# Attention on one Trainium2 core: the inverse deviation of the next image on GpSimd in pieces, half of one value product a round earlier, two norms moved towards each other

## The chip, the cores and the metric

The program runs on one core of a Trainium2 chip. The metric is the device time of one execution in microseconds, taken as the median of several runs. All data are float32.

## What is computed

The input is 8 images of 128 channels by 32 x 32 places. Two layers follow each other; the change lies in the attention of the first.

```python
# x: (8, 128, 32, 32); 8 heads of 16 channels
h = ln_c(x)                                  # over channels: (x - mean) / sqrt(var + 1e-6)
q, k, v = h @ wq.T, h @ wk.T, h @ wv.T
weights = softmax(einsum('bhwnd,bxynd->bnhwxy', q, k) * scale, axis=-1)   # over y only
x = x + einsum('bnhwxy,bxynd->bhwnd', weights, v)
t = x as 1024 tokens of 128
t = t + spectral(ln_t(t))                    # 16 causal filters, ln_t over channels, eps 1e-5
x = x + deformable_conv(ln_c(x))
t = t + experts(ln_t(t))                     # 8 experts, 2 per token
```

The softmax runs over rows of 32 keys, so each query has 32 sums per head.

## The kernel before

**Order.** `metaformer_kernel` first bounds the scores; with the given weights it takes `attention_bounded`, which works with no maximum in the softmax. It writes x1 to DRAM (`x1d`). Then `spectral_and_second_layer` does the spectral filters of image pairs on TensorE and runs the second layer of finished images behind them. Inside the attention the order on every engine is written by hand: `at(round_no, order, ...)` collects pieces, which are issued sorted by round, then by order, then as they were listed. An engine executes its own pieces strictly in that order, and waits at the head of its queue.

**Rounds and units.** An image has 8 units: 4 quarters of 256 queries (`qc`) by 2 groups of 4 heads (`hg`). A unit takes four rounds, so image b begins in round `first` = 32 b and there are 256 rounds. I number them 0 to 255, and call a round's place in its unit its place 0, 1, 2 or 3 (the round number modulo 4). For the unit that starts in round t0:

- Rounds t0 to t0+3, order 0: `scores`, 8 matmuls into the one PSUM tile `s` (L601; the pool has one buffer, 4 banks) and the exponential on ScalarE into `e` (L606). Order 1: `add_tiles` on GpSimd adds the two key tiles to `t` (L615).
- Round t0+5, order 4: `sums`, 16 matmuls into `z` (L622), and on VectorE `reciprocals` (L629).
- Round t0+6, order 2.5: `spread_out`, 4 matmuls into `rb` (L636).
- Rounds t0+6 to t0+9, order 3: `divide` on VectorE, `e` times `rb` (L643).
- Rounds t0+8 to t0+11, order 2: `values`, 8 matmuls into `av` (L653).
- After every second unit `take` copies `av` to `o` (L663, round t0+11), and `results` (L670, round t0+12) transposes it back, so `po` falls in place 0.

As the unit of t0+8 comes two units later, one round of the steady state holds on TensorE: scores, values and one more thing: `po` or a projection of the next image in place 0 (four units of eight each), `z` in place 1, `rb` in place 2, a projection in place 3.

**The next image.** Its rows are loaded and transposed (`tokens`, ScalarE copies to `xt`), normalised, transposed again (`channels`) and projected (`keys`, `queries`, `key_values`), in rounds of the image before, at order 5.5 and 6. `layer_norm_pieces` makes the 21 pieces of the norm: `stats` 0 to 7 on VectorE (L79, L80), `guess` (L84 to L89) and three `newton` (L93 to L96) for the inverse deviation by integer guess and Newton steps, `offset` (L99, tile `lp_nm`), all on VectorE and 128 x 8 numbers each, then `norm` 0 to 7 on ScalarE (L104), which need `lp_nm` and `lp_y`. The list `norm_at` gives their rounds: for images 2 to 7 the stats in 29 to 22 rounds ahead of `first`, `guess` in -22, `newton` in -21, -21, -20, `offset` in -20, four `norm` in -19 and four in -18. Image 1 has a list of its own.

**The first group.** `FirstGroup.pieces` uses the same pieces at order 7 to normalise x1 of images 0 and 1 for the spectral stage (tiles `xc` and `ht`), in rounds 224 + 8 and on for image 0 (`guess` 16, `offset` 20, `norm` 20 to 23) and ten rounds later for image 1, so that its last `norm` come after the last scores.

**Elsewhere.** `inverse_std` does the same computation for later groups of the spectral stage, there with the Newton steps on GpSimd (L757 to L762).

Of the kernel before, what the change touches and what calls it, by code (L numbers as in the profile page):

```python
# [12 lines left out]
I32 = mybir.dt.int32  # L13
AF = mybir.ActivationFunctionType
ALU = mybir.AluOpType
# [3 lines left out]
P = 128  # L19
# [3 lines left out]
NT = T // P  # L23
# [41 lines left out]
def layer_norm_pieces(nc, pool, src, dst, eps):  # L65

    t = {}

    def stats(i):
        if i == 0:
            for name, shape in (
                ("st", [P, NT, 6]), ("mv", [P, NT, 2]), ("v", [P, NT]), ("y", [P, NT]),
                ("w", [P, NT]), ("nm", [P, NT]),
            ):
                t[name] = pool.tile(shape, F32, tag=f"lp_{name}", name=f"lp_{name}")
            t["b"] = pool.tile([P, NT], I32, tag="lp_b", name="lp_b")
        nc.vector.bn_stats(t["st"][:, i, :], src()[:, i, :])  # L79
        nc.vector.bn_aggr(t["mv"][:, i, :], t["st"][:, i, :])  # L80

    def guess():
        v, y = t["v"], t["y"]
        nc.vector.tensor_scalar(v, t["mv"][:, :, 1], eps, None, ALU.add)  # L84
        nc.vector.tensor_scalar(t["b"], v.bitcast(I32), 1, None, ALU.logical_shift_right)
        nc.vector.tensor_scalar(
            y.bitcast(I32), t["b"], -1, 0x5F3759DF, ALU.mult, ALU.add
        )
        nc.vector.tensor_scalar(v, v, -0.5, None, ALU.mult)  # L89

    def newton():
        v, y, w = t["v"], t["y"], t["w"]
        nc.vector.tensor_mul(w, y, y)  # L93
        nc.vector.tensor_mul(w, w, v)
        nc.vector.tensor_scalar(w, w, 1.5, None, ALU.add)
        nc.vector.tensor_mul(y, y, w)  # L96

    def offset():
        nc.vector.scalar_tensor_tensor(  # L99
            t["nm"], t["mv"][:, :, 0], -1.0, t["y"], ALU.mult, ALU.mult  # L100
        )

    def norm(i):
        nc.scalar.activation(  # L104
            dst()[:, i, :], src()[:, i, :], AF.Identity, bias=t["nm"][:, i : i + 1],
            scale=t["y"][:, i : i + 1],
        )

    return (
        [partial(stats, i) for i in range(NT)] + [guess, newton, newton, newton, offset]  # L110
        + [partial(norm, i) for i in range(NT)]
    )
# [379 lines left out]
def attention_bounded(ctx, tc, ident, x, x1d, given, begin_group):  # L492
# [8 lines left out]
    nc = tc.nc  # L501
# [17 lines left out]
    for i in range(2):  # L519
        v = cp.tile([P, NT, VB], F32, name=f"vt{i}")  # L520
# [123 lines left out]
            e, e, un["rb"].unsqueeze(2).to_broadcast([P, NH, 2, QU]), ALU.mult  # L644
        )

    def values(img, un, r, qrt):
        hg = un["at"][1]
        if hg == 0 and r == 0:
            qrt["av"] = rp.tile([P, 512], F32, tag="av", name="av")  # L650
        for c in range(2):
            for j in range(NH):
                nc.tensor.matmul(  # L653
                    qrt["av"][32 * j : 32 * j + 32, 0:QU],
                    img["v"][:, 2 * r + c, P * hg + 32 * j : P * hg + 32 * j + 32],
                    un["e", r][:, j, c, :],
                    start=(hg == 0 and r == 0 and c == 0),
                    stop=(hg == HG - 1 and r == 3 and c == 1), skip_group_check=True,
                )
# [24 lines left out]
    def at(round_no, order, do, *args):  # L684
        work.append((round_no, order, len(work), do, args))

    def spread_rounds(pieces, rounds):
        for piece, round_no in zip(pieces, rounds):
            at(round_no, 6, piece)

    for b in range(B):
        img = {}
        first = 4 * UNITS * b
        project = [
            (keys, img, 0, 0), (keys, img, 0, 1), (queries, img, 0, 0),
            (keys, img, 1, 0), (keys, img, 1, 1), (queries, img, 1, 0),
            (key_values, b, img, 0), (key_values, b, img, 1),
            (queries, img, 0, 1), (queries, img, 1, 1),
        ]
        if b == 0:  # L700
            turn = {"tokens": (0, 0)}
            project_at = (-1, -1, -1, 1, 2, 3, 7, 8, 11, 12)
        else:
            project_at = [first + n for n in (-12, -9, -5, -4, -1, 3, 4, 7, 11, 12)]
            if b == 1:
                turn = {"load": 0, "tokens": (4, 6)}
                norm_at = (5,) * 4 + (7,) * 4 + (8, 8, 9, 9, 9) + (10,) * 4 + (11,) * 4
            else:
                turn = {"load": first - 36, "tokens": (first - 30, first - 26)}
                norm_at = [first - n for n in (  # L710
                    29, 28, 27, 26, 25, 24, 23, 22, 22, 21, 21, 20, 20, 19, 19, 19, 19, 18, 18, 18, 18
                )]
            turn["channels"] = (first - 17, first - 13)
        if b:
            at(turn["load"], 6, load, b)
            spread_rounds(
                layer_norm_pieces(nc, sb, lambda i=img: i["xt"], lambda: given.ht, 1e-6), norm_at
            )
            for par in range(2):
                at(turn["channels"][par], 5.5, channels, par)  # L720
        for par in range(2):
            at(turn["tokens"][par], 5.5, tokens, img, par)
        for step, when in zip(project, project_at):
            at(when, 6, *step)
        for qc in range(QC):
            qrt = {}
            for hg in range(HG):
                un = {"at": (qc, hg)}
                t0 = first + 4 * (HG * qc + hg)
                for r in range(4):  # L730
                    at(t0 + r, 0, scores, img, un, r)
                    at(t0 + r, 1, add_tiles, un, r)
                    at(t0 + 5, 4, sums, un, r)
                    at(t0 + 6 + r, 3, divide, un, r)
                    at(t0 + 8 + r, 2, values, img, un, r, qrt)
                at(t0 + 5, 5, reciprocals, un)
                at(t0 + 6, 2.5, spread_out, un)
            at(t0 + 11, 5, take, qrt)
            at(t0 + 12, 6, results, b, img, qc, qrt)
# [427 lines left out]
class FirstGroup:  # L1167
# [19 lines left out]
    def pieces(self, pool):  # L1187

        got = [(14, self.read), (3, partial(self.load, 0)), (4, partial(self.load, 1))]
        for n in range(2):  # L1190
            pieces = layer_norm_pieces(
                self.nc, pool, lambda n=n: self.ur[n], lambda n=n: self.ur[n], 1e-5
            )
            rounds = [*range(8, 21), *(20 + i // 2 for i in range(8))]
            got += [(r + 10 * n, piece) for r, piece in zip(rounds, pieces)]
        return got


# [258 lines left out]
def metaformer_kernel(  # L1457
# [25 lines left out]
    with tc.If(bounded > P - 1) as branch:  # L1483
        with ExitStack() as part:
            attention_bounded(part, tc, ident, x, x1d, given, begin.pieces)
# [66 lines left out]
```

## Time and profile before

| | |
|---|---|
| median of 3 runs | 3130.27 us (3128.75 to 3132.58) |
| the profiled execution | 3137.39 us, span 3135.6 us |
| attention: first scores to first filter matmul (`pu`) | 27.9 to 996.6 us |
| granted TensorE clock, mean | 0.947 |

The span is what the profile sees of its one execution, 1.8 us less than that execution's time; this execution lies 7.1 us above the median. A timeline line reads: start, duration, engine, line, operation, out<-in, size, count, and in brackets how long the engine was idle before and what released it. A float32 matmul appears as two records, so the 8 matmuls of `scores` are x16. PEld is TensorE's weight load.

### The profile page before, as it was taken

How to read it: one execution, taken by the hardware profiler on the slowest of the kernel's cores; microseconds unless marked ns; L12 is line 12 of the kernel's file. 1: busy time of each engine (PE TensorE's matmuls, PEld its weight loads, DVE VectorE, ACT ScalarE, POOL GpSimd, SP SyncE). 2: the span in 40 equal slices, each digit the busy share in tenths (PEclk: the TensorE clock that was granted, in tenths of full speed). 3: DMA queues.
4: the chain of work that ended last, by engine and by line, in shares of the span. 5: the costliest groups of instructions: out<-in, count | busy, mean ns of one | idle time of the engine just before them, and what ended most of it. 6: DMA issues, size and time to landing. Idle time of an engine off the chain costs nothing.

```text
span 3135.6 us, 45294 instructions
## 1 busy us (share of the span) xinstructions
PE 2793.4 (89%) x18896; PEld 1713.5 (55%) x18896; DVE 1464.0 (47%) x3035; ACT 978.7 (31%) x1198; POOL 957.2 (31%) x800
## 2 busy tenths in 40 slices
PE   7989889989986999999899899899899989899506
PEld 3545445545443666666566566566566656566202
DVE  4788788788786200000522440333522143332487
ACT  4666666666653111112112112212112211111100
POOL 4767667667663200000301300300300030300230
PEclk9999999999998999999999999999899999999758
DMA  0000000000001422210614411511611341610540
GB/s 25 2 15 15 1 15 15 2 15 9 2 28 40 115 61 65 76 48 27 201 41 124 124 34 41 171 58 58 184 34 48 107 121 34 191 51 14 175 146 14
DMA packets 177011, 199.80 MB, mean 64 GB/s; under 512 B 17236, under 2 KB 135188, under 8 KB 176800
## 3 DMA queue, kind: packets, MB, share of 16 engines
q1 hardware_dynamic: 147328, 134.97, 14.4%
q0 software_dynamic: 16800, 55.59, 5.8%
q10 hardware_dynamic: 12672, 6.29, 0.7%
q8 instruction: 150, 2.46, 0.3%
q14 instruction: 61, 0.50, 0.1%
HBM read 128.88 MB, written 67.92 MB: 63 GB/s over the span
## 4 chain that ended last, share of the span: by engine, by line
PE 54%; DVE 4%; another core or an unknown queue 3%; issue 1%; DMA 1%; ACT 1%; POOL 0%; ACTq 0%; POOLq 0%; DVEq 0%
PE pu L1355 33%; PE po L1343 15%; PE p_e L1076 3%; DVE x L1058 2%; PE p_g L1002 1%; DVE x L1082 1%; DMA tab<-gs 1%; PE p_out L1093 0%; PE p_out L1096 0%; PE p_turn L905 0%; PE p_l L1120 0%; DMA g<-tab,cn_idx 0%; ACT us L1359 0%; PE p_ut L1299 0%
## 5 line engine op out<-in xcount | busy, mean ns | idle before, releaser
L1359 ACT COPY us<-pu 128x512 f32<-128x512 f32 x512 | 300.1, 586 | 1382.0 <-PE pu L1355 1228.9
L615 POOL TENSOR_TENSOR t<-e 128x1024 f32<-128x1024 f32 x256 | 620.1, 2424 | 312.2 <-ACT e L606 312.2
L1355 PE MATMUL pu<-teto,ur 128*128 128x512 f32 (+3 forms) x2048 | 603.1, 438 | 51.3 <-ACT us L1359 40.1
L643 DVE TENSOR_TENSOR e<-e,rb 128x2048 f32<-128x2048 f32 x256 | 572.7, 2277 | 87.9 <-PE rb L636 85.6
L606 ACT ACTIVATE e<-s 128x2048 f32<-128x2048 f32 x256 | 480.9, 1878 | 293.2 <-PE s L601 291.6
L1355 PEld LDWEIGHTS pu<-teto,ur 128*128 128x128 f32 x2048 | 390.2, 192 | 330.7 <-issue 201.5
L1343 PE MATMUL po<-us,mf 128*128 128x128 f32 (+2 forms) x2048 | 530.8, 383 | 0.0
L601 PE MATMUL s<-q,k 32*128 32x256 f32 x4096 | 303.0, 411 | 37.0 <-ACT e L606 30.1
L1355 PE MATMUL pu<-teto,ht 128*128 128x512 f32 x992 | 292.2, 438 | 23.0 <-ACT us L1359 23.0
L653 PE MATMUL av<-e,vt 128*32 128x256 f32 x4096 | 283.2, 395 | 28.7 <-DVE e L643 23.8
L1043 POOL DMA_INDIRECT g<-tab,cn_idx x192 | 185.0, 964 | 377.2 <-DMA tab<-gs 194.3
L1355 PE MATMUL pu<-teto,xc 128*128 128x512 f32 x992 | 290.1, 435 | 2.9 <-issue 2.9
L1058 DVE SCALAR_TENSOR_TENSOR x<-g,w,x 128x128 f32<-128x128 f32 x704 | 250.3, 357 | 60.0 <-DVE x L1058 24.1
L601 PEld LDWEIGHTS s<-q,k 32*128 32x128 f32 x4096 | 190.2, 189 | 157.8 <-ACT e L606 101.2
L1355 PEld LDWEIGHTS pu<-teto,xc 128*128 128x128 f32 x992 | 188.7, 191 | 157.0 <-issue 116.9
L1343 PEld LDWEIGHTS po<-us,mf 128*128 128x128 f32 x2048 | 272.1, 193 | 4.1 <-issue 3.9
L757 POOL TENSOR_SCALAR rs_v<-rs_v 128x8 f32<-128x8 f32 x18 | 4.4, 246 | 875.2 <-DVE rs_b L755 875.2
L1082 DVE SCALAR_TENSOR_TENSOR x<-p_e,gates,x 128x128 f32<-128x128 f32 x512 | 177.6, 350 | 187.0 <-PE p_e L1076 170.8
L1355 PEld LDWEIGHTS pu<-teto,ht 128*128 128x128 f32 x992 | 189.6, 192 | 135.7 <-issue 67.0
L653 PEld LDWEIGHTS av<-e,vt 128*32 128x32 f32 x4096 | 108.9, 111 | 164.3 <-issue 72.7
L629 DVE RECIPROCAL r<-z 128x256 f32<-128x256 f32 x64 | 112.4, 1757 | 110.8 <-PE z L622 77.4
L1076 PE MATMUL p_e<-ew,tc 128*128 128x512 f32 x256 | 134.8, 633 | 14.0 <-DVE x L1082 8.9
(235 smaller groups left out, 1809.6 us busy)
## 6 DMA issues: line engine op xcount, KB each, us to landing
tab<-gs SPq DMA_DIRECT2D x168, 256.0 KB
mf<-mfd SPq DMA_DIRECT2D x48, 512.0 KB
teto<-in_phi_o SPq DMA_DIRECT2D x63, 256.5 KB
teto<-in_phi_e SPq DMA_DIRECT2D x63, 256.0 KB
mfd<-mf SPq DMA_DIRECT2D x16, 512.0 KB
tab<-gs ACTq DMA_DIRECT2D x24, 256.0 KB
xc<-in_x SPq DMA_DIRECT2D x8, 512.0 KB
x1d<-xt SPq DMA_DIRECT2D x8, 512.0 KB
```

What stands on the lines that cost most here:

```text
L601: nc.tensor.matmul(s[:, j, c, :], img["k"][rows, hg, 2 * r + c, :], q[rows, qc * QU : (qc + 1) * QU], start=True, stop=True,)
L606: nc.scalar.activation(e.rearrange("p j c q -> p (j c q)"), s.rearrange("p j c q -> p (j c q)"), AF.Exp, scale=float(HD) ** -0.5,)
L615: nc.gpsimd.tensor_add(t, e[:, :, 0, :], e[:, :, 1, :])
L643: nc.vector.tensor_tensor(e, e, un["rb"].unsqueeze(2).to_broadcast([P, NH, 2, QU]), ALU.mult)
L653: nc.tensor.matmul(qrt["av"][32 * j : 32 * j + 32, 0:QU], img["v"][:, 2 * r + c, P * hg + 32 * j : P * hg + 32 * j + 32], un["e", r][:, j, ...
L1043: nc.gpsimd.indirect_dma_start(out=g, out_offset=None, in_=rows, in_offset=bass.IndirectOffsetOnAxis(ap=idx[:, i, tap : tap + 1], axis=0),)
L1058: nc.vector.scalar_tensor_tensor(x3[:, i, :], fetched[n][:, k * C : (k + 1) * C], w[:, i, tap, k : k + 1], (tok if tap + k == 0 else x3)[: ...
L1076: nc.tensor.matmul(pe, tc[:, i * P : (i + 1) * P], self.ew[:, grp * 4 : grp * 4 + 4, :].rearrange("d e c -> d (e c)"), start=True, stop=True,)
L1082: nc.vector.scalar_tensor_tensor(x3[:, i, :], pe[:, k * C : (k + 1) * C], gate[:, i, grp * 4 + k : grp * 4 + k + 1], x3[:, i, :], ALU.mult ...
L1343: self.nc.tensor.matmul(out, lhsT, rhs, start=bank not in group["opened"], stop=last, skip_group_check=True)
L1355: nc.tensor.matmul(pu[:, i * P : HT], group["ur"][n][:, src * 4 + i, :], flt[:, 0 : HT - i * P], start=(i == 0), stop=(i == 3),)
L1359: nc.scalar.copy(us[:, n, :], pu)
```

## The change

Three edits.

1. `guess`, `newton` and `offset` are issued on GpSimd. The guess no longer shifts the bits: it multiplies the integer by -0.5 and adds the constant in one operation, so the tile `lp_b` goes; `offset` becomes two operations. On VectorE these were 17 operations (4 + 12 + 1), on GpSimd they are 17 (3 + 12 + 2). The rounds for images 2 to 7 change: stats in pairs in -29, -28, -25, -24, `guess` in -24, `newton` in -23, -22, -22, `offset` in -22, `norm` in pairs in -21 to -18. Image 1 keeps its rounds.
2. `values` takes the key tiles it is to do. For r = 1 the first half (4 matmuls) moves from round t0+9 to the end of round t0+8 (order 6.5, behind projections and `po`).
3. In the first group, image 1's norm follows image 0's by 4 rounds instead of 10.

```diff
     def guess():
         v, y = t["v"], t["y"]
-        nc.vector.tensor_scalar(v, t["mv"][:, :, 1], eps, None, ALU.add)
-        nc.vector.tensor_scalar(t["b"], v.bitcast(I32), 1, None, ALU.logical_shift_right)
-        nc.vector.tensor_scalar(
-            y.bitcast(I32), t["b"], -1, 0x5F3759DF, ALU.mult, ALU.add
-        )
-        nc.vector.tensor_scalar(v, v, -0.5, None, ALU.mult)
+        nc.gpsimd.tensor_scalar(v, t["mv"][:, :, 1], eps, None, ALU.add)
+        nc.gpsimd.tensor_scalar(
+            y.bitcast(I32), v.bitcast(I32), -0.5, 0x5F3759DF, ALU.mult, ALU.add
+        )
+        nc.gpsimd.tensor_scalar(v, v, -0.5, None, ALU.mult)
     def newton():
         v, y, w = t["v"], t["y"], t["w"]
-        nc.vector.tensor_mul(w, y, y)
+        nc.gpsimd.tensor_mul(w, y, y)
...
     def offset():
-        nc.vector.scalar_tensor_tensor(
-            t["nm"], t["mv"][:, :, 0], -1.0, t["y"], ALU.mult, ALU.mult
-        )
+        nc.gpsimd.tensor_mul(t["nm"], t["mv"][:, :, 0], t["y"])
+        nc.gpsimd.tensor_scalar(t["nm"], t["nm"], -1.0, None, ALU.mult)
...
-    def values(img, un, r, qrt):
+    def values(img, un, r, cs, qrt):
...
-        for c in range(2):
+        for c in cs:
...
                 norm_at = [first - n for n in (
-                    29, 28, 27, 26, 25, 24, 23, 22, 22, 21, 21, 20, 20, 19, 19, 19, 19, 18, 18, 18, 18
+                    29, 29, 28, 28, 25, 25, 24, 24, 24, 23, 22, 22, 22, 21, 21, 20, 20, 19, 19, 18, 18
                 )]
...
-                    at(t0 + 8 + r, 2, values, img, un, r, qrt)
+                at(t0 + 8, 2, values, img, un, 0, (0, 1), qrt)
+                at(t0 + 8, 6.5, values, img, un, 1, (0,), qrt)
+                at(t0 + 9, 2, values, img, un, 1, (1,), qrt)
+                at(t0 + 10, 2, values, img, un, 2, (0, 1), qrt)
+                at(t0 + 11, 2, values, img, un, 3, (0, 1), qrt)
...
-            got += [(r + 10 * n, piece) for r, piece in zip(rounds, pieces)]
+            got += [(r + 4 * n, piece) for r, piece in zip(rounds, pieces)]
```

More of the change, by code (lines that the diff above doesn't have):

```diff
@@ L77, in stats @@
                 t[name] = pool.tile(shape, F32, tag=f"lp_{name}", name=f"lp_{name}")
-            t["b"] = pool.tile([P, NT], I32, tag="lp_b", name="lp_b")
         nc.vector.bn_stats(t["st"][:, i, :], src()[:, i, :])
@@ L83, in guess @@
         v, y = t["v"], t["y"]
-        nc.vector.tensor_scalar(v, t["mv"][:, :, 1], eps, None, ALU.add)
-        nc.vector.tensor_scalar(t["b"], v.bitcast(I32), 1, None, ALU.logical_shift_right)
-        nc.vector.tensor_scalar(
-            y.bitcast(I32), t["b"], -1, 0x5F3759DF, ALU.mult, ALU.add
+        nc.gpsimd.tensor_scalar(v, t["mv"][:, :, 1], eps, None, ALU.add)
+        nc.gpsimd.tensor_scalar(
+            y.bitcast(I32), v.bitcast(I32), -0.5, 0x5F3759DF, ALU.mult, ALU.add
         )
-        nc.vector.tensor_scalar(v, v, -0.5, None, ALU.mult)
+        nc.gpsimd.tensor_scalar(v, v, -0.5, None, ALU.mult)
     def newton():
         v, y, w = t["v"], t["y"], t["w"]
-        nc.vector.tensor_mul(w, y, y)
-        nc.vector.tensor_mul(w, w, v)
-        nc.vector.tensor_scalar(w, w, 1.5, None, ALU.add)
-        nc.vector.tensor_mul(y, y, w)
+        nc.gpsimd.tensor_mul(w, y, y)
+        nc.gpsimd.tensor_mul(w, w, v)
+        nc.gpsimd.tensor_scalar(w, w, 1.5, None, ALU.add)
+        nc.gpsimd.tensor_mul(y, y, w)
     def offset():
-        nc.vector.scalar_tensor_tensor(
-            t["nm"], t["mv"][:, :, 0], -1.0, t["y"], ALU.mult, ALU.mult
-        )
+        nc.gpsimd.tensor_mul(t["nm"], t["mv"][:, :, 0], t["y"])
+        nc.gpsimd.tensor_scalar(t["nm"], t["nm"], -1.0, None, ALU.mult)
     def norm(i):
```

## The prediction

> **What bounds the kernel now.** I read the busy slices of the page first: from 100 us to 900 us, inside the attention, TensorE is busy for eight to ten tenths of each slice, VectorE for seven or eight. The groups say what it does there, and the times at which successive `scores` start say how evenly. They are 3.17 us apart in places 0, 2 and 3 and 3.80 in place 1, so a unit takes 13.3 us. Two things set this. In places 0, 2 and 3 it is a loop through one PSUM tile: scores until their exponential starts 1.26, exponential 1.88, start of the next scores. In place 1 it is TensorE itself: scores 1.07, values 0.89, `z` 1.84 make 3.80. Nine times that rhythm breaks; the timeline of one break (image 2's norm):
>
> ```profile
> 187.41 2.38 DVE L86 TENSOR_SCALAR lp_y<-lp_b 128x8 int32<-128x8 int32 x1
> ...
> 190.41 1.15 PE L601 MATMUL s<-q,k 32*128 32x256 f32 x16
> ...
> 193.72 2.41 POOL L615 TENSOR_TENSOR t<-e 128x1024 f32<-128x1024 f32 x1 [0.80 <-ACT e L606]
> 193.78 2.37 DVE L94 TENSOR_TENSOR lp_w<-lp_w,lp_v 128x8 f32<-128x8 f32 x1
> ...
> 194.82 1.15 PE L601 MATMUL s<-q,k 32*128 32x256 f32 x16
> ...
> 198.81 1.74 PE L653 MATMUL av<-e,vt 128*32 128x256 f32 x16 [2.84 <-DVE e L643]
> ...
> 199.74 1.66 ACT L104 ACTIVATE ht<-xt,lp_nm,lp_y 128x128 f32<-128x128 f32 x4 [6.16 <-DVE lp_nm L99]
> ...
> 201.76 1.75 DVE L629 RECIPROCAL r<-z 128x256 f32<-128x256 f32 x1
> ...
> 203.56 2.08 PE L636 MATMUL rb<-r,spread 64*128 64x256 f32 x8 [3.02 <-DVE r L629]
> 205.57 2.09 PE L601 MATMUL s<-q,k 32*128 32x256 f32 x16
> ```
>
> Two tiny VectorE operations of 0.17 us take 2.4, ending when GpSimd's add ends; with the other 15 they push the divides and the reciprocal back. ScalarE stands 6.16 us at the `norm` for `lp_nm`, the exponential queued behind it. TensorE waits for the divide, then for the reciprocal, and runs at half clock afterwards (scores 2.09 for 1.15). The next scores start 10.75 us later. The waits inside the attention add it up:
>
> ```profile
> ACT ht L104 <- DVE lp_nm L99: 44.2, 8, 6.3
> ```
>
> Over the rhythm, the gaps for image 2 (rounds 45 to 48) are 4.41 + 10.75 + 4.43 - (3.80 + 3.17 + 3.17) = 9.5 us; the others alike at 320, 438, 671 and 789 us; image 5 6.9 (550 us). Image 1 loses 7.1 (gaps 8.00, 4.56, 4.05 against 3.17, 3.17, 3.20 at 73 us); the first group 9.7 (4.23, 8.65, 5.80, 4.35 between 915 and 965 us against 3.17, 3.80, 3.17, 3.17). The nine sum to 71.
>
> **What the skill says.** "SBUF — State Buffer", "Who interferes with whom": a VectorE operation with two SBUF inputs, or a `tensor_scalar` in its two-port mode, and a GpSimd operation that reads SBUF exclude each other for a whole instruction; one with at most one SBUF input, outside such a mode, doesn't contend. The trace agrees: 2.37 above beside GpSimd's 2.41, while divides (one input in PSUM) take 2.28 beside the same adds. "TensorE: Matmul & The Clock Gate", "What's actually happening": the clock halves after about 3.4 us of idleness and comes back after as much work. Here 2.84 us idle was followed by 2.09 for 1.15.
>
> **The change part by part.**
>
> **GpSimd's price.** The trace has such operations, later, on the same 128x8 shape:
>
> ```profile
> 1076.19 0.19 POOL L759 TENSOR_TENSOR rs_t<-rs_y 128x8 f32<-128x8 f32 x1
> 1076.46 0.20 POOL L760 TENSOR_TENSOR rs_t<-rs_t,rs_v 128x8 f32<-128x8 f32 x1
> 1076.75 0.25 POOL L761 TENSOR_SCALAR rs_t<-rs_t 128x8 f32<-128x8 f32 x1
> 1077.08 0.20 POOL L762 TENSOR_TENSOR rs_y<-rs_y,rs_t 128x8 f32<-128x8 f32 x1
> 1077.36 0.20 POOL L759 TENSOR_TENSOR rs_t<-rs_y 128x8 f32<-128x8 f32 x1
> ```
>
> One step of 4 is 1.17 us, 0.29 an operation; 17 are 5.0 us. No row shows the integer one: between 0.25 and, as an estimate, 1.0 (four times the `tensor_scalar`); I take 0.29. GpSimd's adds take 2.43 of a 3.17 round, so 5.0 us is a backlog of some 7 rounds' spare 0.74.
>
> **Images 2 to 7.** VectorE loses 17 operations per image (17 x 0.17 = 2.9 us, up to 7 with the waits) and no longer meets GpSimd. I walk image 2, with time 0 at the scores of round 39 (place 3). VectorE: divides 0.18 to 4.6, two stats (0.43 each) to 5.5, divide 7.7, two stats to 8.6, divide 10.8. GpSimd: add of round 40 until 8.9, guess 9.8, add(41) 12.2, newton 13.4, add(42) 15.8, two newtons and offset (10 operations) 18.7, add(43) 21.1. Behind the wait for the stats stands add(41); `z` of round 45 needs add(43) at about 22, so it is met by 1 us. Three things remain:
> - Four stats instead of two lie between the divides of each of two units. The reciprocal starts at 10.8 where `z` ends at 9.9; `rb` and the next scores come 0.9 later, in the other unit 0.3 (its place 0 carries a projection).
> - Round 43's exponential ends at 16.9, the query copy 17.5, then ScalarE waits 1.3 for `lp_nm`; two norms (0.43 each) to 19.7; exponential 44 starts 1.5 late. TensorE had 0.5 to spare there: 1.0.
>
> So 2.2 per image against 5 x 9.5 + 6.9 = 54.4: 54.4 - 13.2 = **41 less**. Bounds: no stall left (54 less), or the half clock back in each, some 2.3 more each (27 less).
>
> **Image 1** keeps its rounds: guess and a newton after add(8) (65.9 us on the old clock), add(9) 68.3, ten operations 71.2; four norms then hold exponential 11 from 69.5 to 73. Scores 12 and 13 come 1.3 to 2.7 earlier: **2 less** (0 to 4).
>
> **First group.** `offset` and the first norms share a round. Add(244) starts when exponential 244 ends (plus 0.6 backlog), takes 2.43, offset 0.6; two norms 0.85: exponential 245 is 3.2 late, TensorE 3.0, and half clock after it, 1.9 (from the 1.26 to 2.63 of rounds 47 and 246). Twice: 9.8; late reciprocals in two units that now hold up to five stats more 1.8. 11.6 against 9.7: **2 more** (5 less to 5 more).
>
> **The tail.** Today image 1's last norms stand ahead of `o` on ScalarE (5.29 us) and TensorE waits 4.85 for it; from scores 255 (964.36) to `pu` (996.64) are 32.3. Without them VectorE runs on: four divides to 9.1 after scores 255, reciprocal 10.8, `rb` 12.0, four divides 21.1, values 22.1, and from `o` to `pu` 4.0 as now (992.60 to 996.64): 26.2. **6 less** (4 to 7).
>
> **The half values.** Half is 0.89 / 2 = 0.445. Place 1 falls from 3.80 to 3.36. With `po` in place 0, TensorE has 1.07 + 1.00 + 0.66 = 2.73 of 3.17; the half fits (3.18). With a projection (1.12) place 0 is full at 3.20 and grows to 3.64. So it pays in 30 of the units, 0.33 to 0.44 each, and a further switch of tile may cost 28 others 0.05: 11.4 - 1.4 = **10 less** (5 to 13). Divide 1 is done at 4.6 to 5.5, the half is reached at 5.9.
>
> SP's queue is unchanged; GpSimd's two indirect loads keep their rounds. What follows the attention starts from its end and moves with it.
>
> **Sum.** -41 - 2 + 2 - 6 - 10 = -57. The profiled execution, 3137.4, would take 3080; it lies 7.1 above the median, so 3130.3 - 57 = **3073**.
>
> **Rivals.**
> - *lp_nm as late as before (20%)*: backlog on GpSimd (every add 2.43 of 3.17) keeps ScalarE waiting some 4 us per norm and the half clock stays; images then yield 27 and the halves 5: about 3098. For: `offset` one round ahead of `norm`. Against: seven fewer rounds of VectorE queue.
> - *Better than walked (12%)*: stats hidden, no half clock in the first group: 12 to 15 less, about 3060.
> - *Slower (5%)*: small GpSimd operations, dispatched between adds and beside divides, stretch. 57 us over nine norms is 6.3 each, over 17 operations 0.37: from 0.66 us an operation on the gain is gone. At 0.8 the norms cost 17 x 0.51 x 9 = 78: 3151. The rows above, at 0.29, speak against it.
> - *No effect (3%)*: another wait of equal length hides behind `lp_nm`; nothing in the waits shows one.
>
> **Numbers.** Main case 60%, 3060 to 3088. Range 3054 to 3104 takes in the first two rivals. Faster by over 0.2% (6 us, about what a measurement can tell from none) 0.91, within 0.03, slower 0.06.
>
> **What would show it.** Place 1 at 3.36 and place 0 with `po` at about 3.18; no gap over 5 us for images 2 to 7; ScalarE's wait for `lp_nm` near 1.3 there and 3 to 4 in the first group; GpSimd's 17 operations near 0.2 each; `pu` at about 940. If VectorE's reciprocal is late without stats before it, or `z` waits for an add, the walk is wrong.

## The result and the profile after

| | before | after |
|---|---|---|
| median of the runs | 3131.43 us (3128.75 to 3137.65, 4 runs) | 3090.53 us (3088.33 to 3094.10, 4 runs) |
| ratio, 95% interval | | 0.9868 (0.9849 to 0.9886) |
| the profiled execution, its span | 3137.39, 3135.6 us | 3088.59, 3086.6 us |
| first scores to first filter matmul | 968.7 us | 926.0 us |

The change makes the kernel 41 us faster; the forecast was 57. At 3090.5 it lies inside the range given, 3054 to 3104, and 2.5 above the main case, 3060 to 3088.

I call the last row of the table the stretch. In one trace it can be read to 0.1 us, while whole executions of one kernel differ by several us. Where two kernels issue the same operations, their rounds mostly repeat as closely: the first 236 rounds take 863.3 us in before and in "near alone" below. They do not always: after a stall, TensorE's half clock came in some traces and not, or later, in others (last section), which moved equal rounds by 1.3 to 2.6 us. So a difference under 3 us between two traces can be the clock's and not an edit's. The stretch fell by 42.7. What follows it took 2140.8 us of the profiled execution before and 2134.6 after; over the ten kernels profiled here it lies between 2130 and 2141, and the changes end where it begins, so I count none of that for the change.

The waits inside the attention, in the changed kernel (us in total, times, longest). The line numbers are those of the changed file.

```profile
ACT ht L101 <- POOL lp_nm L98: 28.5, 8, 3.8
ACT xc L101 <- POOL lp_nm L98: 3.2, 1, 3.2
```

The wait of `ht` for `lp_nm` went from 44.2 to 28.5 and its longest from 6.3 to 3.8, that of `xc` (the first group) from 6.0 to 3.2. I had expected 1.3 for each of images 2 to 7. The timeline of image 2's norm, on the part of it that answers to the break shown before:

```profile
173.56 2.37 POOL L612 TENSOR_TENSOR t<-e 128x1024 f32<-128x1024 f32 x1 [0.79 <-ACT e L603]
...
174.75 0.18 DVE L79 BATCH_NORM_AGGREGATE lp_mv<-lp_st 128x2 f32<-128x6 f32 x1
...
175.88 2.37 POOL L675 TENSOR_TENSOR xt<-xt,at 128x1024 f32<-128x1024 f32 x1
...
178.34 0.24 POOL L83 TENSOR_SCALAR lp_v<-lp_mv 128x8 f32<-128x8 f32 x1
178.65 0.20 POOL L84 TENSOR_SCALAR lp_y<-lp_v 128x8 int32<-128x8 int32 x1
...
187.43 0.24 POOL L98 TENSOR_SCALAR lp_nm<-lp_nm 128x8 f32<-128x8 f32 x1
187.63 2.35 POOL L612 TENSOR_TENSOR t<-e 128x1024 f32<-128x1024 f32 x1
187.70 0.88 ACT L101 ACTIVATE ht<-xt,lp_nm,lp_y 128x128 f32<-128x128 f32 x2 [3.75 <-POOL lp_nm L98]
188.49 1.85 ACT L603 ACTIVATE e<-s 128x2048 f32<-128x2048 f32 x1
...
190.39 2.09 PE L598 MATMUL s<-q,k 32*128 32x256 f32 x16 [3.33 <-ACT e L603]
...
195.35 1.15 PE L598 MATMUL s<-q,k 32*128 32x256 f32 x16
```

Three things are to be seen. No GpSimd operation of the norm is stretched: 0.20 to 0.24, the integer one 0.20, and 0.19 to 0.26 over all nine norms. The stats were done at 174.93, but the guess began at 178.34: between the add of round 40 and the guess stands `xt + at` (L675, 2.37 us), the end of image 0, which `results` issues in round 40. And TensorE, idle for 3.33, came back at half clock: scores 2.09 for 1.15, while the next ones took 1.15 again.

The trace of before has the same add, 7.4 us ahead of a guess that then stood on another engine:

```profile
179.57 2.37 POOL L678 TENSOR_TENSOR xt<-xt,at 128x1024 f32<-128x1024 f32 x1
...
186.99 0.17 DVE L84 TENSOR_SCALAR lp_v<-lp_mv 128x8 f32<-128x8 f32 x1
```

### The profile page after: what moved, and what is told of

Same layout as the page of the kernel before. It is cut to its first block, busy times and chain, and to the rows that moved or that the text cites. A ratio compares the mean times of both kernels' runs of the same rounds, so it can differ in the third digit from the quotient of the medians.

```text
span 3086.6 us, 45238 instructions
## 1 busy us (share of the span) xinstructions
PE 2781.7 (90%) x18896; PEld 1699.8 (55%) x18896; DVE 1402.5 (45%) x2882; ACT 976.6 (32%) x1198; POOL 974.5 (32%) x953
## 4 chain that ended last, share of the span: by engine, by line
PE 55%; DVE 5%; issue 3%; another core or an unknown queue 2%; DMA 1%; ACT 0%; POOL 0%; ACTq 0%; POOLq 0%; DVEq 0%
PE pu L1356 34%; PE po L1344 15%; PE p_e L1077 3%; DVE x L1059 2%; PE p_g L1003 1%; DVE x L1083 1%; DMA tab<-gs 1%; PE p_out L1097 0%; PE p_out L1094 0%; PE p_turn L906 0%; PE p_l L1121 0%; ACT us L1360 0%; PE p_ut L1300 0%; PE p_back L1110 0%
## 5 line engine op out<-in xcount | busy, mean ns | idle before, releaser
L612 POOL TENSOR_TENSOR t<-e 128x1024 f32<-128x1024 f32 x256 | 607.2, 2372 | 243.0 <-ACT e L603 242.7
L650 PE MATMUL av<-e,vt 128*32 128x256 f32 x4096 | 292.2, 393 | 4.8 <-DVE e L640 3.5
L650 PEld LDWEIGHTS av<-e,vt 128*32 128x32 f32 x4096 | 101.6, 110 | 149.4 <-issue 90.7
```

Of the source, the lines that this page charges most:

```text
L612: nc.gpsimd.tensor_add(t, e[:, :, 0, :], e[:, :, 1, :])
L650: nc.tensor.matmul(qrt["av"][32 * j : 32 * j + 32, 0:QU], img["v"][:, 2 * r + c, P * hg + 32 * j : P * hg + 32 * j + 32], un["e", r][:, j, ...
```

## The experiments

Each kernel's trace is read alike: for images 2 to 7, the 12 rounds from first-26 to first-15 (the norm and two units around it); for image 1, rounds 8 to 14; for the first group, rounds 236 to 254; the tail from scores 255 to `pu`. "Rest" is what is left of the stretch. In us:

| kernel | stretch | image 1 | images 2 to 7, each | first group | rest | tail |
|---|---|---|---|---|---|---|
| before | 968.7 | 30.6 | 50 (image 5: 47.5) | 73.1 | 535.6 | 32.3 |
| after | 926.0 | 28.1 | 45.0 | 69.5 | 532.0 | 26.2 |
| halves alone | 955.6 | 29.8 | 48.7 (47.0) | 70.3 | 532.7 | 32.1 |
| norm alone | 936.9 | 28.0 | 45.7 to 46.9 | 65.5 | 534.9 | 30.5 |
| near alone | 962.9 | 30.6 | 50 (47.5) | 71.5 | 535.6 | 28.1 |
| end-of-image add later | 903.7 | 29.5 | 41.2 | 69.7 | 530.7 | 26.4 |
| VectorE, new rounds | 977.1 | 31.1 | 51.0 to 52.0 | 70.5 | 535.1 | 32.2 |
| GpSimd, old rounds | 917.0 | 28.1 | 42.6 to 43.6 | 70.7 | 532.0 | 27.5 |
| norms later | 899.0 | 28.1 | 40.5 | 69.6 | 532.0 | 26.3 |
| all later | 884.0 | 23.7 | 40.1 | 63.6 | 528.6 | 27.6 |

**The three edits, one at a time.** Halves alone is the kernel before with the diff's `values` and its five `at` lines; norm alone is `layer_norm_pieces` and the new `norm_at`; near alone is one number:

```diff
-            got += [(r + 10 * n, piece) for r, piece in zip(rounds, pieces)]
+            got += [(r + 4 * n, piece) for r, piece in zip(rounds, pieces)]
```

> The kernel before with edit 2 alone. Measured on the trace as the stretch from the first scores to the first filter matmul: 968.7 us before, 926.0 after. From the gaps of the changed kernel (place 1 at 3.37 for 3.80; place 0 with po 3.29 for 3.17, with a projection 3.70 for 3.17) 30 units gain 0.32 and 28 lose 0.10: 6.8 less, 962. The prediction's sum said 10 less, 959. If the half products only paid because they ran beside the new norm, under 3 less.

Measured: 955.6, 13.1 less, time 3121.29 in one run. More than any of the three. The gaps outside the breaks are those of the changed kernel, so about 7 of it is the steady gain, as expected; the other 6 come out of the breaks. The 12 rounds of images 2 to 7 fall by 1.1 on average, of which 0.5 is steady gain. The first group falls by 2.8, but round 246 alone, where before ran at half clock and this kernel did not, gives 2.6 (5.80 to 3.23).

> The kernel before with edit 1 alone (GpSimd and the new rounds; the first group's two norms ten rounds apart as before, the values whole). If the three edits add up: what the norms of images 1 to 7 gained in the changed kernel, about 2.7 + 27 = 30 less, tail unchanged: 939, with round first-20 again over 6.5 us for images 2 to 7. If the norm's gain needs the shorter place 1, 945 or more.

Measured: 936.9, 31.8 less, time 3102.36. Close to the first case (939) in total, with round first-20 at 6.85. But the tail shrank by 1.8, and the first group by 7.6 (2.6 of it round 246 again, now 3.17), which I had not counted.

> The kernel before with edit 3 alone (two norms four rounds apart, still on VectorE). Tail from scores 255 to the filter matmul 26.2 instead of 32.3, as no norm stands behind the last scores. In the loop two chains of 17 VectorE operations now follow each other with stats between: if VectorE's stretched operations are what hurts, the 9.7 lost there stay or grow to some 14. Together 2 to 6 less: 963 to 967.

Measured: 962.9, 5.8 less, as expected in total and not in its parts: tail 28.1 (4.2 less, not 6.1), the first group 1.6 less. But the first group's gain is not the edit's. The scores of round 246 come after the same stall in before and in near alone, at half clock in the first and at full clock in the second:

```profile
930.69 2.09 PE L601 MATMUL s<-q,k 32*128 32x256 f32 x16 [3.23 <-ACT e L606]
...
931.27 1.15 PE L601 MATMUL s<-q,k 32*128 32x256 f32 x16 [3.23 <-ACT e L606]
```

That round takes 5.80 in before and 3.23 here. "VectorE, new rounds" below has before's first group unchanged, and without the half clock it takes 70.5. Against that, near alone makes the first group 1.0 longer, inside what I had expected, and the edit saves some 3 us. Its time in one run, 3131.16, can't be told from before.

Alone the three give 13.1 + 31.8 + 5.8 = 50.7, together 42.7. The tail adds up (1.8 and 4.2 alone, 6.1 together); the first group does not: 2.8 + 7.6 + 1.6 alone, 3.6 together. Each of these four figures holds the 2.6 of before's round 246. Without it the three give 42.9 and all together 40.1, so little overlap is left.

**The add ahead of the guess.** The suspected step, moved and nothing else:

```diff
-        if qc == QC - 1:
-            nc.gpsimd.tensor_add(img["xt"], img["xt"], img["at"])
-            nc.sync.dma_start(x1d[b], img["xt"])
+        if qc == QC - 1 and b == B - 1:
+            store(b, img)
+
+    def store(b, img):
+        nc.gpsimd.tensor_add(img["xt"], img["xt"], img["at"])
+        nc.sync.dma_start(x1d[b], img["xt"])
...
             at(t0 + 12, 6, results, b, img, qc, qrt)
+            if qc == QC - 1 and b < B - 1:
+                at(t0 + 18, 1.5, store, b, img)
```

> The changed kernel with one move: the add of xt and at on GpSimd (2.37 us, with the store behind it) at the end of images 0 to 6 six rounds later, so it no longer stands ahead of the next norm's guess. Theory A (that add is the step my walk left out): lp_nm is ready 2.4 earlier, ScalarE waits about 1.4 instead of 3.75 for it, TensorE doesn't fall to half clock in round first-19, images 2 to 7 lose 2.2 each instead of 5: stretch about 909, time some 17 less than the changed kernel. Rival B (the backlog comes from the key adds and the 17 operations themselves): the wait stays over 3, under 4 less in all. Rival C (the add only moves the backlog to where z or the values wait): wait gone but the same time.

Measured: stretch 903.7, 22.3 less than the changed kernel; 3072.83 us median of 4, ratio to before 0.9819 (0.9803 to 0.9836) against 0.9868 (0.9849 to 0.9886). Theory A holds: its timeline has

```profile
173.49 2.38 POOL L612 TENSOR_TENSOR t<-e 128x1024 f32<-128x1024 f32 x1 [0.79 <-ACT e L603]
...
175.95 0.24 POOL L83 TENSOR_SCALAR lp_v<-lp_mv 128x8 f32<-128x8 f32 x1
...
185.35 0.88 ACT L101 ACTIVATE ht<-xt,lp_nm,lp_y 128x128 f32<-128x128 f32 x2 [1.47 <-POOL lp_nm L98]
...
188.04 1.15 PE L598 MATMUL s<-q,k 32*128 32x256 f32 x16 [1.05 <-ACT e L603]
```

The guess starts when the key add ends, the wait is 1.47, TensorE idles 1.05 and stays at full clock. The loss of a norm is 4.81 - 3.70 = 1.1, where I had expected 2.2; in the changed kernel it was 7.10 + 4.96 - 3.70 - 3.37 = 5.0. So 2.3 of a later `lp_nm` cost 3.9, the half clock among it. Images 2 to 7 take 22.7 less in all. Image 1 is 1.4 longer than in the changed kernel and the first two rounds are 1.3 shorter, although this edit touches neither: TensorE's half clock begins and ends at other moments there (scores of round 1 at 1.15 for 2.09 in the changed kernel, of round 12 at 2.09 for 1.83).

**Engine or rounds.** There are two lists of rounds and two engines, and two of the four combinations have not been shown yet. The first kernel below makes this edit to the kernel before; the second makes the reverse of it to the changed kernel:

```diff
-    29, 28, 27, 26, 25, 24, 23, 22, 22, 21, 21, 20, 20, 19, 19, 19, 19, 18, 18, 18, 18
+    29, 29, 28, 28, 25, 25, 24, 24, 24, 23, 22, 22, 22, 21, 21, 20, 20, 19, 19, 18, 18
```

> The kernel before with the new list of rounds alone, everything still on VectorE. Theory (VectorE's operations meet GpSimd's adds and push divides and reciprocal back): the loss stays, 12 rounds around a norm take 48 to 52 us (50 before, 45 after), stretch 960 to 975. Rival (the rounds make the gain, the engine doesn't matter): 45 or less per norm, stretch about 940.

Measured: 977.1, 8.4 more than before and 2 above my bracket; 51.0 to 52.0 per norm. The rounds alone do harm. On VectorE the guess meets the end-of-image add too:

```profile
178.70 1.03 DVE L84 TENSOR_SCALAR lp_v<-lp_mv 128x8 f32<-128x8 f32 x1
...
179.65 2.39 POOL L678 TENSOR_TENSOR xt<-xt,at 128x1024 f32<-128x1024 f32 x1
179.77 2.29 DVE L85 TENSOR_SCALAR lp_b<-lp_v 128x8 int32<-128x8 int32 x1
...
181.98 4.71 POOL L615 TENSOR_TENSOR t<-e 128x1024 f32<-128x1024 f32 x2
...
182.10 2.32 DVE L86 TENSOR_SCALAR lp_y<-lp_b 128x8 int32<-128x8 int32 x1
...
184.33 2.38 DVE L89 TENSOR_SCALAR lp_v<-lp_v 128x8 f32<-128x8 f32 x1
...
188.82 1.74 DVE L629 RECIPROCAL r<-z 128x256 f32<-128x256 f32 x1
...
190.62 2.08 PE L636 MATMUL rb<-r,spread 64*128 64x256 f32 x8 [7.46 <-DVE lp_w L93]
```

GpSimd had three adds back to back, and three VectorE operations of 0.17 took 2.29 to 2.38, each ending with one of them. The reciprocal and a divide stood behind; TensorE waited 7.46 at `rb`, which reads it. (The bracket names `lp_w`, the small operation that starts just before; `rb` reads `r`, which was ready at 190.56.)

> The changed kernel with the old list of rounds for images 2 to 7. The end-of-image add is then two rounds ahead of the guess, but offset only one round ahead of four norms in a row: lp_nm about 2.7 after ScalarE wants it, the next exponential 2.9 late, half clock: 45 per norm as in the changed kernel, stretch 920 to 932. If the old rounds are better than the new, under 43 per norm.

Measured: 917.0, 9 less than the changed kernel, and 42.6 to 43.6 per norm; 45 was wrong.

```profile
183.07 0.24 POOL L83 TENSOR_SCALAR lp_v<-lp_mv 128x8 f32<-128x8 f32 x1 [0.19 <-DVE lp_mv L79]
...
192.50 1.65 ACT L101 ACTIVATE ht<-xt,lp_nm,lp_y 128x128 f32<-128x128 f32 x4 [2.37 <-POOL lp_nm L98]
...
195.96 1.15 PE L598 MATMUL s<-q,k 32*128 32x256 f32 x16 [2.42 <-ACT e L603]
```

The guess now follows the last stats and no longer waits for the end-of-image add. ScalarE waits 2.37, near the 2.7 expected, but TensorE idles 2.4 instead of 3.33, and the half clock that I had counted on stays away at images 2, 4 and 6. At images 3, 5 and 7 it comes late in the round, behind part or all of the scores (values 1.93, 1.93 and 1.70 for 1.07), and costs 1 us. So GpSimd with the old rounds beats GpSimd with the new ones, and of edit 1 the engine makes the gain (with the new rounds 977.1 on VectorE, against 936.9 on GpSimd in norm alone) and the new rounds, as they stand, give some back.

**Asking later.** The opposite of making `lp_nm` earlier: the same kernel, the norms one round later.

```diff
-    ..., 22, 22, 22, 21, 21, 20, 20, 19, 19, 18, 18
+    ..., 22, 22, 22, 20, 20, 19, 19, 18, 18, 17, 17
```

> The changed kernel with only the eight norm operations of images 2 to 7 one round later; the end-of-image add stays ahead of the guess. Theory A (ScalarE held by lp_nm that is 2.4 late): lp_nm then comes 0.7 after it is wanted, the next exponential 0.3 late: 40.5 per norm instead of 45, no half clock, stretch about 898. Rival C (the late add hurts elsewhere, at z): 43 or more.

Measured: 899.0 and 40.5 per norm, as theory A says, 27.0 less; 3064.81 in one run. The end-of-image add is where it was, so the lateness did no harm but through ScalarE:

```profile
186.99 1.15 PE L598 MATMUL s<-q,k 32*128 32x256 f32 x16
187.47 0.24 POOL L98 TENSOR_SCALAR lp_nm<-lp_nm 128x8 f32<-128x8 f32 x1
187.74 0.88 ACT L101 ACTIVATE ht<-xt,lp_nm,lp_y 128x128 f32<-128x128 f32 x2 [0.63 <-POOL lp_nm L98]
188.53 1.85 ACT L603 ACTIVATE e<-s 128x2048 f32<-128x2048 f32 x1
...
190.67 1.15 PE L598 MATMUL s<-q,k 32*128 32x256 f32 x16
```

`lp_nm` is ready at 187.7, the same moment as in the changed kernel. Only it is now asked for after the next exponential has been let through.

**Everything together.** The two moves of above, the norms of image 1 and of the first group later too, and the half values only in units whose place 0 holds `po`:

```diff
-    norm_at = (5,) * 4 + (7,) * 4 + (8, 8, 9, 9, 9) + (10,) * 4 + (11,) * 4
+    norm_at = (5,) * 4 + (7,) * 4 + (8, 8, 9, 9, 9) + (11, 11, 12, 12, 13, 13, 14, 14)
...
-                at(t0 + 8, 6.5, values, img, un, 1, (0,), qrt)
-                at(t0 + 9, 2, values, img, un, 1, (1,), qrt)
+                if hg == 0:
+                    at(t0 + 8, 6.5, values, img, un, 1, (0,), qrt)
+                at(t0 + 9, 2, values, img, un, 1, (1,) if hg == 0 else (0, 1), qrt)
...
-            rounds = [*range(8, 21), *(20 + i // 2 for i in range(8))]
+            rounds = [*range(8, 21), *(22 + i // 2 for i in range(8))]
```

> The changed kernel with the add six rounds later, the norms of images 2 to 7 one round later, those of image 1 from round 11 in pairs, those of the first group two rounds later, and the half values moved only where place 0 holds po. If all that was left is ScalarE held by lp_nm and 0.10 per unit with a projection: 40.1 per norm, image 1 25, first group 62, stretch 880 to 888, time about 3048.

Measured: stretch 884.0; 3048.80 us median of 4 (3042.14 to 3054.76), ratio to before 0.9733 (0.9715 to 0.9751). It beats both kernels. Its waits hold no line with `lp_nm` any more. Image 1 is at 23.7, the first group at 63.6, 1.6 more than expected. Of that, 0.85 lies in round 242, which still takes 4.02: two stats and a divide stand ahead of the reciprocal, and `rb` waits 0.81 for it.

## Why the prediction was right, and where its size was off

- **The bound and the nine breaks**: right. Outside the breaks the gaps of before and after agree to a few hundredths, apart from places 0 and 1. With the wait for `lp_nm` gone altogether (all later), images 2 to 7 take 40.1 instead of 50. The halves save 0.6 of that there; the other 9.3 are nearly the 9.5 that I had read off the gaps.
- **GpSimd's price**: right. 0.20 to 0.24 an operation, the integer one 0.20 (L84); newton from 181.45 to 182.54. The slower rival had no ground.
- **Images 2 to 7, 41 less**: the mis-sized term. Measured 50 - 45.0 per norm, 297.1 to 270.1 for the six; without the 0.5 each that the halves save in those rounds, 24 less. The step that failed is "add of round 40 until 8.9, guess 9.8": GpSimd had another 2.37 us to do, the end-of-image add of `results`, which the trace of before shows in the same round. I had read SP's queue and the indirect loads for what is ahead of the norm, and not this. `lp_nm` came 20.5 after scores 39 instead of 18.7, ScalarE waited 3.75 instead of 1.3, and the idle time brought the half clock; round 44 took 7.1, where I had said none over 5. I had named this as a bound ("half clock back in each", 27 less); the outcome lies somewhat beyond it.
- **The late reciprocal, 0.9 and 0.3**: wrong, but small. In rounds 38 to 43 there was no delay: round 38 also holds `tokens`, so the divides had started half a us before the scores of round 39 (166.64 against 167.13), not 0.18 after. With the add moved away a norm cost 1.1, against 1.0 for the ScalarE term alone.
- **Image 1**: 2.7 of excess less; predicted 2. **Tail**: 26.2, as predicted. VectorE's eight divides and the reciprocal set it, as in the walk.
- **First group, 2 more**: 9.7 became 7.6 of excess over the rhythm (round 242 0.85, round 245 2.47, rounds 249 and 250 2.73 and 1.56). The wrong sign comes from before: 2.6 of the 9.7 is the half clock of round 246, which the same operations with the same stall did not have in two other traces. Against 7.1 without it, 7.6 is 0.5 more. The waits for `lp_nm` were 3.2 and 3.3, as I had said, but TensorE idled 2.39 after the first, which did not bring the half clock, where I had charged 1.9 for it, and 2.66 after the second, which did (1.56).
- **Halves, 10 less**: place 1 came out at 3.37 (predicted 3.36), place 0 with `po` at 3.29 (3.18), with a projection 3.70 (3.64). The half costs 0.06 to 0.11 more than its share of the matmuls. The further switch of tile that I had put at 0.05 would do that, but no run separates it. 30 x 0.32 - 28 x 0.10 = 6.8.
- **Sum**: 24 + 2.7 + 2.1 + 6.1 + 6.8 = 41.7 of 42.7, against 57. Some luck is in how near it came: the late reciprocals (1.2 per norm, 7 in all) and the first group (4) were put too high, and made up for part of what the add and the halves cost. Without these two errors I would have said some 68 less.
- **Rivals**: the likeliest, `lp_nm` late again, was half of the truth. It had the wait (about 4 us, with the half clock), and named GpSimd's backlog but not the add that made it. Its own terms (27, 2, 6 and 5 less, 2 more) sum to 38 less, 3092, and not to its 3098.

Open: halves alone takes another 6 out of the breaks of the kernel before. The half clock of round 246 is 2.6 of it. In the break of image 2, `lp_nm` is ready 12.0 us after the scores of round 44 instead of 12.4, and the reciprocal ends 15.9 after them instead of 16.3: the one Newton operation that then ends with an add takes 1.95 instead of 2.37. How the rest arises, no run separates.

## What to carry to other kernels

When a step moves to another engine, list everything that engine does in those rounds, also what occurs once per image, and not only its steady work: here one add of 2.37 us per image ahead of 17 small operations cost 22 us where 43 were gained. A wait at the head of an in-order queue costs by what is queued behind it, so asking one round later (one exponential let through) was worth at least as much (27 us) as having the answer 2.3 us sooner (22). A stall of TensorE of around 3 us may bring the half clock, which here cost 1.0 to 2.9 us more than the stall. Before a difference of that size between two traces is put down to an edit, see whether the same operations ran at the same clock in both.

## What I had not expected of the hardware

- The length of a stall does not decide whether TensorE's half clock follows. After 3.23 us idle in round 246, scores took 2.09 in before and 1.15 in near alone and in "VectorE, new rounds", and the round 5.80 or 3.23. After 2.81 us idle in round 12, the same scores took 2.09 in "end-of-image add later", 1.80 in "norms later" and 1.19 in "GpSimd, old rounds", where the values behind them slowed to 1.94. In the changed kernel the half clock came after 3.33, 2.79 and 2.66 us (scores 2.09, 1.83, 1.78) and not after 2.39 (1.15). In the break of before that the prediction shows, 2.84 us idle slowed the values (1.74 for 1.07), and the scores of 2.09 came after a second wait of 3.02. "TensorE: Matmul & The Clock Gate", "What's actually happening", calls the window of about 3.4 us free-running, which fits that equal stalls end differently. That a whole idle window of this length is needed, as I had taken from it, does not fit: stalls of 2.4 to 2.8 us were enough here, and the measurement decides.
- Four matmuls split off a group of eight cost 0.53 us where they went and saved 0.43 where they were: the gap of place 0 with a projection grew from 3.17 to 3.70, place 1 fell from 3.80 to 3.37.
